# Routing logits of a mixture-of-experts layer taken from the sum ahead of the layer norm

## The chip, the cores and the metric

The kernel runs on one core of one Trainium2 chip, as one program. The metric is device time in microseconds (us), from the start of the program to its end. A run with the hardware profiler gives, beside its time, a trace of what every engine did: TensorE (PE, with its weight loads as PEld), VectorE (DVE), ScalarE (ACT), GpSimd (POOL), and SyncE (SP), which issues most of the DMA transfers.

## The reference

Two transformer layers stand one behind the other. The tensor is 8 x 1024 tokens of 256 values, all in float32. The first layer is an attention over the 16 heads of each token; the second is an attention over the first axis (8 positions, for each of 1024 columns), a layer norm, and a mixture of experts with 8 experts, a capacity of 1024 tokens each, and the best expert for each token. Cut to what matters here:

```python
x  = layernorm(x + first_attention(x))                      # phase A
o  = attention(x)                                           # 4 heads of 64, over 8 positions
y1 = _ln(x + o @ ow.T + ob, ln1_g, ln1_b)                   # eps 1e-5
gates = softmax(y1 @ wg)                                    # wg is 256 x 8
idx   = argmax(gates);  gate_val = gates[idx]
slot  = idx * cap + (rank of the token among those of its expert)   # dropped where rank >= cap
y2 = _ln(y1 + gate_val * expert(idx)(y1), ln2_g, ln2_b)
out = layernorm(x + y2)
```

The logits are `y1 @ wg`. With `s = x + o @ ow.T + ob` for the sum ahead of the norm, mean m and rs = 1/sqrt(var + eps), y1 is `(s - m) * rs * ln1_g + ln1_b`. So with `w = ln1_g * wg` and w centred (the mean over the 256 rows taken off each of its 8 columns), the logits are also `rs * (s @ w) + ln1_b @ wg`: the mean of s falls out, and `s @ w` is the sum of `x @ w`, `o @ (ow.T @ w)` and `ob @ w`.

## The kernel before

The program has three phases. Phase A (`phase_a`) computes the first layer, 64 tiles of 128 tokens, and writes x to DRAM (`x1_d`). Phase B (`phase_b`) computes the second attention, the first norm and the routing. Phase C (`phase_c`) finds each token's place, gathers the rows of each expert, multiplies them, normalises twice and scatters the result.

Phase B works in 8 groups `j` of 128 columns with all 8 positions (`L = 8`), 1024 tokens each. The order of its work is written out by hand. Round `j` has four parts `n`; each computes the attention scores of one quarter (`scores`: matmuls on PE, their maximum `mx` on DVE), the exponentials on ACT (`weights`, two halves), their normalisation (`normed`, DVE), and then, one part later, the turned weights (`turn_s`: transposes on PE, copy `sT` on ACT) and the weighted product (`weighted`: PE, copy `oT` on ACT). Between these steps the list from `fills(j)` is worked off: `some(1)` takes one entry behind the scores, `some(2)` takes two behind the turn, and the rest comes behind `weighted`. In the first part an `output` is held back until `weighted` of the part before is done.

The fills of round j are of two groups. For the next group, `nxt`: `turn_x` turns x with transposes on PE into the PSUM pool `fill` (three buffers) and copies it to `xT` on DVE, in the order that the attention needs; `project_qk` and `project_v` multiply it by the weights. For the group before, `prv`: `output(j, l0)` multiplies two positions of the attention's result by `wout` into one tile of `fill`, POOL makes `xb` = x + out_b (`residual`), DVE adds the two to `r` and takes mean and variance, and POOL makes `rs` (`norm_scalars`). `normal(j, l0)` makes y on DVE, multiplies it by ln1_g and adds ln1_b on POOL, adds ln2_b to x for the later norm on POOL, and sends both rows to `rows_d` in DRAM through SP. `turn_y` turns y on PE and copies it (`yT`) on ACT, `logits` multiplies it by `wg`, and after the last of them `exps` and `choice` compute the softmax, the gate and the expert of the 1024 tokens. `choice` sends the gate column to `rows_d`. `expert_bias` accumulates the bias part of one expert on DVE in rounds 0 to 5; in round 7 the products of two experts are fills.

Each engine works its queue in the order in which the program issues it. A DMA also waits for the transfer eight places before it, which used the same of eight semaphores. Rounds j = -1 (setup: group 0 is turned and projected) and j = 8 (tail: outputs, norms and routing of group 7, with no scores beside them) frame the eight.

Of the kernel before, what the change touches and what calls it, by code (L numbers as in the profile page):

```python
# [24 lines left out]
FP = mybir.dt.float32  # L25
# [8 lines left out]
P = 128  # L34
D = 256
# [14 lines left out]
@with_exitstack  # L50
def fused_kernel(ctx: ExitStack, tc: tile.TileContext, a: dict, out: bass.AP):
    nc = tc.nc

    const = ctx.enter_context(tc.tile_pool(name="const", bufs=1))
    small = ctx.enter_context(tc.tile_pool(name="small", bufs=4))

    ident = const.tile([P, P], FP, name="ident")
    make_identity(nc, ident)
    mhalf = const.tile([P, 1], FP, name="mhalf")
    nc.gpsimd.memset(mhalf, -0.5)  # L60

    dram = ctx.enter_context(tc.tile_pool(name="dram", bufs=1, space=bass.MemoryType.DRAM))
    x1_d = dram.tile([L * N, D], FP, name="x1_d")
    rows_d = dram.tile([L * N, RW], FP, name="rows_d")

    def norm_scalars(r):

        st = small.tile([P, 6], FP, name="st")
        nc.vector.bn_stats(out=st, in_=r)
        mv = small.tile([P, 2], FP, name="mv")  # L70
        nc.vector.bn_aggr(out=mv, in_=st)  # L71
        ve = small.tile([P, 1], FP, name="ve")
        nc.gpsimd.tensor_scalar(ve, mv[:, 1:2], EPS, None, ALU.add)  # L73
        rs = small.tile([P, 1], FP, name="rs")
        nc.gpsimd.tensor_tensor(rs, ve, mhalf, ALU.pow)
        return mv[:, 0:1], rs

    phase_a(tc, a, ident, x1_d, norm_scalars)

    late = ctx.enter_context(tc.tile_pool(name="late", bufs=1))  # L80
    keep = {
        "w12": late.tile([P, DC, E, D], FP, name="w12"),

        "acc": late.tile([P, E, D], FP, name="acc"),
        "hot": late.tile([P, E, NT], FP, name="hot"),
        "gain": late.tile([P, D], FP, name="gain"),
        "red": late.tile([P, NT], FP, name="red"),
    }
    constants(nc, late, keep)
    nc.scalar.dma_start(keep["gain"], a["ln2_g"].partition_broadcast(P))  # L90
    phase_b(tc, a, ident, x1_d, rows_d, keep, norm_scalars)
    phase_c(tc, a, ident, rows_d, keep, out)

# [447 lines left out]
def phase_b(tc, a, ident, x1_d, rows_d, keep, norm_scalars):  # L541
# [8 lines left out]
    with (  # L550
# [15 lines left out]
        for n in ("in_b_v", "out_b", "ln1_g", "ln1_b", "ln2_b"):  # L566
            rows[n] = wp.tile([P, D], FP, name=f"row_{n}")
            nc.scalar.dma_start(rows[n], a[n].partition_broadcast(P))
        wout = wp.tile([P, DC, D], FP, name="wout")
        nc.sync.dma_start(wout, a["out_wT"].rearrange("(c p) f -> p c f", p=P))  # L570
        wg = wp.tile([P, DC, E], FP, name="wg")
        nc.sync.dma_start(wg, a["wg"].rearrange("(c p) e -> p c e", p=P))
        b1 = wp.tile([P, FC, E], FP, name="b1")
# [19 lines left out]
        hot_v = keep["hot"].rearrange("p e (l j) -> p j l e", j=NJ)  # L593
        red_v = keep["red"].rearrange("p (l j) -> p j l", j=NJ)

        def load_x(j):
            G["x", j] = xp.tile([P, L, D], FP, name="x")
            nc.sync.dma_start(G["x", j], x1_v[j])

        def turn_x(j, l0):  # L600
            if l0 == 0:
                G["xT", j] = wp.tile([P, DC, NB, L, B], FP, name="xT")
                G["qk", j] = gp.tile([P, DC, 2, N], FP, name="qk")
            ps = pf.tile([P, 512], FP, name="fill")
            for l in range(2):
                for c in range(DC):
                    n = 2 * l + c
                    nc.tensor.transpose(
                        ps[:, n * P : (n + 1) * P], G["x", j][:, l0 + l, c * P : (c + 1) * P], ident
                    )  # L610
            for l in range(2):
                nc.vector.tensor_copy(
                    G["xT", j][:, :, :, l0 + l, :],
                    ps[:, l * D : (l + 1) * D].rearrange("p (c b n) -> p c b n", c=DC, n=B),
                )
# [118 lines left out]
            )  # L734
            return xb

        def output(j, l0):
            xb = residual(j, l0)
            ps = pf.tile([P, 512], FP, name="fill")
            for l in range(2):  # L740
                for c in range(DC):
                    nc.tensor.matmul(
                        ps[:, l * D : (l + 1) * D],
                        G["oT", j][:, c, l0 + l, :],
                        wout[:, c, :],
                        start=c == 0,
                        stop=c == DC - 1,
                    )
            r = kp.tile([P, 2, D], FP, name="r")
            nc.vector.tensor_tensor(r, ps.rearrange("p (l d) -> p l d", l=2), xb, ALU.add)  # L750
            G["r", j, l0] = r, [norm_scalars(r[:, l, :]) for l in range(2)]

        def normal(j, l0):
            r, sc = G["r", j, l0]
            yx = kp.tile([P, 2, 2 * D], FP, name="yx")
            y = yx[:, :, :D]
            G["y", j, l0] = y
            for l in range(2):
                nc.vector.tensor_scalar(y[:, l, :], r[:, l, :], sc[l][0], sc[l][1], ALU.subtract, ALU.mult)
            both = [P, 2, D]  # L760
# [4 lines left out]
            )  # L765
            nc.sync.dma_start(rows_v[j][:, l0 : l0 + 2, : 2 * D], yx)

        def turn_y(j, l0):
            y = G["y", j, l0]
            ps = pf.tile([P, 512], FP, name="fill")  # L770
            for l in range(2):
                for c in range(DC):
                    n = 2 * l + c
                    nc.tensor.transpose(
                        ps[:, n * P : (n + 1) * P], y[:, l, c * P : (c + 1) * P], ident
                    )
            yT = kp.tile([P, 4, P], FP, name="yT")
            nc.scalar.copy(yT, ps)
            G["yT", j, l0] = yT

        def logits(j, l0):
            yT = G["yT", j, l0]
            ps = pf.tile([P, 512], FP, name="fill")
            for l in range(2):
                for c in range(DC):
                    nc.tensor.matmul(
                        ps[:, l * E : (l + 1) * E],
                        yT[:, 2 * l + c, :],
                        wg[:, c, :],
                        start=c == 0,  # L790
                        stop=c == DC - 1,
                    )
            if l0 == 0:
                G["lg", j] = kp.tile([P, L, E], FP, name="lg")
            nc.vector.tensor_copy(
                G["lg", j][:, l0 : l0 + 2, :], ps[:, : 2 * E].rearrange("p (l e) -> p l e", l=2)
            )

        def over_experts(v):
            return v[:, :, None].to_broadcast([P, L, E])  # L800

        def exps(j):
            lg = G["lg", j]
            top = kp.tile([P, L], FP, name="top")
            nc.vector.tensor_reduce(top, lg, AX.X, ALU.max)
            nc.vector.tensor_tensor(lg, lg, over_experts(top), ALU.subtract)
            nc.scalar.activation(lg, lg, AF.Exp)
# [58 lines left out]
        def fills(j):  # L866
# [8 lines left out]
            def put(part, ok, fn, *args):  # L875
                if ok:
                    o[part].append((fn, *args))

            put(0, N, turn_x, nxt, 0)
            put(0, N, turn_x, nxt, 2)  # L880
            put(0, N, turn_x, nxt, 4)
            put(0, O, output, prv, 0)
            put(0, N, turn_x, nxt, 6)
            put(0, O, output, prv, 2)
            put(0, X, expert_bias, EARLY + j, 0)
            put(0, O, normal, prv, 0)
            put(0, N, project_qk, nxt, 0, 0, 0)
            put(1, O, normal, prv, 2)
            put(1, O, turn_y, prv, 0)
            put(1, O, output, prv, 4)  # L890
            put(1, N, project_qk, nxt, 0, 0, 1)
            put(1, O, logits, prv, 0)
            put(1, O, normal, prv, 4)
            put(1, O, turn_y, prv, 2)
            put(1, X, expert_bias, EARLY + j, 1)
            put(1, N, project_v, nxt, 0)
            put(1, O, logits, prv, 2)
            put(1, N, project_qk, nxt, 0, 1, 0)
            put(2, O, turn_y, prv, 4)
            put(2, O, output, prv, 6)  # L900
            put(2, N, project_qk, nxt, 0, 1, 1)
            put(2, O, logits, prv, 4)
            put(2, O, normal, prv, 6)
            put(2, X, expert_bias, EARLY + j, 2)
            put(2, N, project_v, nxt, 2)
            put(2, N, project_qk, nxt, 1, 0, 0)
            put(2, N, project_v, nxt, 4)
            put(3, O, turn_y, prv, 6)
            put(3, N, project_qk, nxt, 1, 0, 1)
            put(3, N, project_v, nxt, 6)  # L910
            put(3, O, logits, prv, 6)
            put(3, O, exps, prv)
            put(3, X, expert_bias, EARLY + j, 3)
            put(3, N, project_qk, nxt, 1, 1, 0)
            put(3, O, choice, prv)
            put(3, N, project_qk, nxt, 1, 1, 1)
            if j == NJ - 1:
                for n in range(4):
# [449 lines left out]
```

## Time and profile before

| | us |
|---|---|
| runs of the kernel before | 5184.34, 5194.05, 5193.99 |
| median | 5193.99 |
| the profiled execution | 5145.15 |
| its span in the trace | 5143.4 |
| PE busy in the span | 4903.2 (95%) |
| DVE, ACT, POOL busy | 3070.0, 3360.9, 3374.4 |
| mean granted clock of TensorE | 0.977 |

A time in the trace counts from the start of the span. A row of the timeline or of a group gives start or count, duration, engine, line of the kernel, operation, the tile written and the tile read, and in brackets the idle time of the engine ahead of it with what ended that. The granted clock is the share of TensorE's full speed that the throttle let through. L numbers are lines of the kernel before.

### The profile page before, as it was taken

How to read it: one execution, taken by the hardware profiler on the slowest of the kernel's cores; microseconds unless marked ns; L12 is line 12 of the kernel's file. 1: busy time of each engine (PE TensorE's matmuls, PEld its weight loads, DVE VectorE, ACT ScalarE, POOL GpSimd, SP SyncE). 2: the span in 40 equal slices, each digit the busy share in tenths (PEclk: the TensorE clock that was granted, in tenths of full speed). 3: DMA queues.
4: the chain of work that ended last, by engine and by line, in shares of the span. 5: the costliest groups of instructions: out<-in, count | busy, mean ns of one | idle time of the engine just before them, and what ended most of it. 6: DMA issues, size and time to landing. Idle time of an engine off the chain costs nothing. (4 is left out here: it accounts for less than half of the span.)

```text
span 5143.4 us, 189684 instructions
## 1 busy us (share of the span) xinstructions
PE 4903.2 (95%) x79688; PEld 3310.9 (64%) x79688; DVE 3070.0 (60%) x6088; ACT 3360.9 (65%) x4123; POOL 3374.4 (66%) x7014
## 2 busy tenths in 40 slices
PE   7999999999999999999999999999999997889675
PEld 4666666666666666666666666666666664566553
DVE  5665655666566666665666656666666563555467
ACT  5777777777777777777777777777777774444234
POOL 5667667677767767766776776776776764254436
PEclk9999999999999999999999999999999998999787
DMA  2222222222222222222222222222222222132253
GB/s 76 47 48 48 48 48 49 47 49 49 46 48 48 47 48 48 49 47 48 49 47 48 49 46 48 48 48 47 48 49 48 49 47 61 48 76 71 66 182 114
DMA packets 575308, 286.29 MB, mean 56 GB/s; under 512 B 394865, under 2 KB 526065, under 8 KB 574449
## 3 DMA queue, kind: packets, MB, share of 16 engines
q1 hardware_dynamic: 365970, 111.51, 10.9%
q0 software_dynamic: 204800, 159.82, 10.4%
q8 instruction: 623, 10.21, 0.8%
q10 hardware_dynamic: 3680, 2.83, 0.2%
q14 instruction: 235, 1.93, 0.1%
HBM read 72.31 MB, written 33.59 MB: 21 GB/s over the span
## 5 line engine op out<-in xcount | busy, mean ns | idle before, releaser
L359 ACT ACTIVATE e<-pair 128x1024 f32<-128x1024 f32 x3072 | 2977.4, 1021 | 1233.0 <-PE pair L343 1233.0
L403 POOL DMA_DIRECT2D nd<-S x4096 | 1952.9, 484 | 613.3 <-DVE S L393 420.9
L343 PE MATMUL pair<-R,L 32*128 32x128 f32 (+1 forms) x32768 | 1605.6, 322 | 2.0 <-POOL event L314 2.0
L393 DVE COPY S<-sum 128x512 f32<-128x512 f32 x1024 | 707.1, 691 | 1465.9 <-PE sum L382 1153.2
L343 PEld LDWEIGHTS pair<-R,L 32*128 32x128 f32 x32768 | 1271.3, 186 | 48.2 <-POOL event L314 2.6
L373 PE MATMUL sum<-e,V 128*32 128x256 f32 x16384 | 1284.9, 385 | 4.9 <-DVE S L393 4.9
L300 POOL DMA_DIRECT2D R<-qm x2048 | 973.8, 483 | 71.7 <-issue 39.2
L382 PE MATMUL sum<-e,V 128*32 128x128 f32 x16384 | 823.3, 273 | 0.0
L382 PEld LDWEIGHTS sum<-e,V 128*32 128x32 f32 x16384 | 532.8, 110 | 352.2 <-issue 0.9
L373 PEld LDWEIGHTS sum<-e,V 128*32 128x32 f32 x16384 | 406.3, 109 | 236.6 <-DVE qm L267 41.8
L331 PE MATMUL pair<-late,sel 32*128 32x256 bf16 (+1 forms) x6144 | 499.3, 313 | 9.6 <-ACT e L359 9.6
L254 DVE COPY V<-vT 32x128 f32<-32x128 f32 x2048 | 457.4, 223 | 28.1
L412 DVE RECIPROCAL att<-nd 128x256 f32<-128x256 f32 x256 | 447.4, 1748 | 8.0 <-DMA nd<-S 4.1
L331 PEld LDWEIGHTS <-sel 32*128 32x128 bf16 x6144 | 155.4, 91 | 460.4 <-issue 445.0
L314 POOL MEMSET event<- 1x1 f32 x256 | 22.8, 89 | 610.9 <-DMA R<-qm 416.4
L234 PEld LDWEIGHTS ps<-xT,wv 128*128 128x128 f32 x2048 | 238.2, 191 | 44.4 <-issue 41.8
L223 PE MATMUL ps<-wk,xT 128*128 128x512 f32 x512 | 255.3, 621 | 10.9 <-DMA wk<-in_Wk 10.1
L234 PE MATMUL ps<-xT,wv 128*128 128x128 f32 x2048 | 262.6, 281 | 1.6 <-DVE qm L267 0.8
L266 PE MATMUL ps<-wq,xT 128*128 128x512 f32 x512 | 255.7, 622 | 6.7 <-DVE k L224 6.7
L443 PE MATMUL ps<-wo,attT 128*128 128x256 f32 x1024 | 257.9, 395 | 0.7 <-ACT attT L426 0.7
L443 PEld LDWEIGHTS ps<-wo,attT 128*128 128x128 f32 x1024 | 186.1, 191 | 63.7 <-issue 41.8
L73 POOL TENSOR_SCALAR ve<-mv 128x1 f32<-128x1 f32 x128 | 37.9, 296 | 271.6 <-DVE mv L71 270.1
(191 smaller groups left out, 3856.0 us busy)
## 6 DMA issues: line engine op xcount, KB each, us to landing
R<-qm POOLq DMA_DIRECT2D x2048, 32.0 KB, 2.1
nd<-S POOLq DMA_DIRECT2D x4096, 16.0 KB, 1.9
L<-k SPq DMA_DIRECT2D x4088, 8.0 KB
rows_d<-yx SPq DMA_DIRECT2D x32, 512.0 KB
xT<-in_xT SPq DMA_DIRECT2D x64, 128.0 KB
xr<-in_x SPq DMA_DIRECT2D x64, 128.0 KB
x_d<-x1o SPq DMA_DIRECT2D x64, 128.0 KB
x<-x_d SPq DMA_DIRECT2D x8, 1024.0 KB
```

Of the source, the lines that this page charges most:

```text
L234: nc.tensor.matmul(ps[:, i * P : (i + 1) * P], w["v"][:, c, ch * P : (ch + 1) * P], xT_of[t][:, c, :], start=c == 0, stop=c == DC - 1,)
L254: nc.vector.tensor_copy(V[32 * aa : 32 * aa + 32, qd % 2, :, qd // 2, :, aa, 0:4], src[32 * qd : 32 * qd + 32, :, ww, :, aa, :],)
L300: moved.append((None, nc.gpsimd.dma_start(R[:, b, s, b, :], q[:, b, s, cols])))
L331: nc.tensor.matmul(bank[u].rearrange("p (n i) -> p n i", i=n)[:, :, 0:32], sel[pr].rearrange("p a j -> p (a j)"), late[pr, None, :].to_bro ...
L343: one = nc.tensor.matmul(bank[u][:, x * 4 * n : (x + 1) * 4 * n].rearrange("p (b i) -> p b i", i=n), Lt[pr, 2 * (h0 + h) + jb].rearrange(" ...
L359: nc.scalar.activation(e, pair[i], AF.Exp)
L373: nc.tensor.matmul(dst[32 * u : 32 * u + 32], Vs[ww][:, 0, h0 + h, u, :], e0[u // 2][:, u % 2, x * 256 : (x + 1) * 256].rearrange("p (b i) ...
L382: nc.tensor.matmul(dst[32 * u : 32 * u + 32, :, 32:], Vs[ww][:, 1, h0 + h, u, :], e1[u // 2][:, u % 2, h * 128 : (h + 1) * 128].rearrange( ...
L393: nc.vector.tensor_copy(S[:, :, 2 * which : 2 * which + 2, :].rearrange("p b h i -> p h b i"), ps.rearrange("p (h b i) -> p h b i", h=2, b=4),
L403: nc.gpsimd.dma_start(tok[:, b, s, h0 * C1 : (h0 + G) * C1], Sx[:, 4 if s else b, b, :])
L412: nc.vector.reciprocal(att[:, cols], nd[:, 1, cols])
L443: nc.tensor.matmul(ps[:, :D], attT[:, c, :], wo[:, c, :], start=c == 0, stop=c == HID // P - 1)
```

## The change

The logits no longer wait for y. Three parts of the sum ahead of the norm give them:

- `center` and `beside`, new, in the setup: w = ln1_g * wg, centred; `out_w` times w goes as eight further columns beside `out_wT` into `wout`; the two constant rows (out_b and ln1_b through w and wg) go to `wrow`. For this `out_w` and three short columns are loaded.
- `turn_x` also keeps x turned in the plain order (`xl`, a copy on ACT of the same PSUM tile), and `logits_x`, new, multiplies it by w and adds the constant row: the part of the logits that x gives, one round ahead.
- `output` now takes one position l at a time; its product has 256 + 8 columns, and DVE adds the eight to `lg`. `rs` goes to one tile for the group, and `exps` multiplies the logits by it and adds the second constant row.
- `turn_y` and `logits` are gone, and with them the copy `yT`. The order of the fills is new. In the tail `normal` of the last pair comes behind `choice`.

Cut to its core:

```diff
-        wout = wp.tile([P, DC, D], FP, name="wout")
-        nc.sync.dma_start(wout, a["out_wT"].rearrange("(c p) f -> p c f", p=P))
+        wout = wp.tile([P, DC, D + E], FP, name="wout")
+        nc.sync.dma_start(wout[:, :, :D], a["out_wT"].rearrange("(c p) f -> p c f", p=P))
+        outw = wp.tile([P, DC, D], FP, name="outw")
+        nc.sync.dma_start(outw, a["out_w"].rearrange("(c p) f -> p c f", p=P))
+        cols = {}
+        for n in ("ln1_g", "ln1_b", "out_b"):
+            cols[n] = wp.tile([P, DC], FP, name=f"col_{n}")
+            nc.scalar.dma_start(cols[n], a[n].rearrange("(c p) -> p c", p=P), allow_slow_non_contiguous=True)
...
+        def center():
+            w = ww[:, :, 0, :]
+            nc.vector.tensor_tensor(w, wg, column("ln1_g"), ALU.mult)
+            ps = pf.tile([P, 512], FP, name="fill")
+            for c in range(DC):
+                nc.tensor.matmul(ps[:, :E], keep["ones"], w[:, c, :], start=c == 0, stop=c == DC - 1)
+            mean = wp.tile([P, E], FP, name="mean")
+            nc.vector.tensor_scalar(mean, ps[:, :E], 1.0 / D, None, ALU.mult)
+            nc.vector.tensor_tensor(w, w, mean[:, None, :].to_broadcast([P, DC, E]), ALU.subtract)
+            nc.vector.tensor_tensor(ww[:, :, 1, :], w, column("out_b"), ALU.mult)
+            nc.vector.tensor_tensor(ww[:, :, 2, :], wg, column("ln1_b"), ALU.mult)
+
+        def beside():
+            ps = pf.tile([P, 512], FP, name="fill")
+            for k in range(DC):
+                for c in range(DC):
+                    nc.tensor.matmul(ps[:, k * E : (k + 1) * E], outw[:, c, k * P : (k + 1) * P], ww[:, c, 0, :], ...)
+            sums = ps[:, DC * E : (DC + 2) * E]
+            for c in range(DC):
+                nc.tensor.matmul(sums, keep["ones"], ww[:, c, 1:, :].rearrange("p k e -> p (k e)"), ...)
+            nc.vector.tensor_copy(wout[:, :, D:], ps[:, : DC * E].rearrange("p (k e) -> p k e", k=DC))
+            nc.vector.tensor_copy(wrow, sums.rearrange("p (k e) -> p k e", k=2))
...
         def turn_x(j, l0):
...
+            xl = kp.tile([P, 4, P], FP, name="xl")
+            nc.scalar.copy(xl, ps)
+            G["xl", j, l0] = xl
             for l in range(2):
                 nc.vector.tensor_copy(
...
+        def logits_x(j, l0):
...
+                    nc.tensor.matmul(ps[:, l * E : (l + 1) * E], G["xl", j, l0][:, 2 * l + c, :], ww[:, c, 0, :], ...)
+            nc.vector.tensor_tensor(G["lg", j][:, l0 : l0 + 2, :], ps[:, : 2 * E]..., wrow[:, 0:1, :]..., ALU.add)
+
+        def output(j, l):
+            if l == 0:
+                G["rs", j] = gp.tile([P, L], FP, name="rs")
+            if l % 2 == 0:
+                G["r", j, l] = kp.tile([P, 2, D], FP, name="r"), residual(j, l), []
+            r, xb, scalars = G["r", j, l - l % 2]
+            r, xb = r[:, l % 2, :], xb[:, l % 2, :]
+            ps = pf.tile([P, 512], FP, name="fill")
+            for c in range(DC):
+                nc.tensor.matmul(ps[:, : D + E], G["oT", j][:, c, l, :], wout[:, c, :], ...)
+            nc.vector.tensor_tensor(r, ps[:, :D], xb, ALU.add)
+            lg = G["lg", j][:, l, :]
+            nc.vector.tensor_tensor(lg, ps[:, D : D + E], lg, ALU.add)
+            scalars.append(norm_scalars(r, G["rs", j][:, l : l + 1]))
...
         def exps(j):
             lg = G["lg", j]
+            nc.vector.tensor_tensor(lg, lg, over_experts(G["rs", j]), ALU.mult)
+            nc.vector.tensor_tensor(lg, lg, wrow[:, None, 1, :].to_broadcast([P, L, E]), ALU.add)
...
+            last = not N and not X and not 0 <= j < NJ
+            put(0, j < 0, center)
             put(0, N, turn_x, nxt, 0)
             put(0, N, turn_x, nxt, 2)
+            put(0, j < 0, beside)
+            put(0, N, logits_x, nxt, 0)
             put(0, N, turn_x, nxt, 4)
+            put(0, N, logits_x, nxt, 2)
             put(0, O, output, prv, 0)
             put(0, N, turn_x, nxt, 6)
-            put(0, O, output, prv, 2)
+            put(0, O, output, prv, 1)
+            put(0, N, logits_x, nxt, 4)
             put(0, X, expert_bias, EARLY + j, 0)
             put(0, O, normal, prv, 0)
             put(0, N, project_qk, nxt, 0, 0, 0)
+            put(0, N, logits_x, nxt, 6)
+            put(0, O, output, prv, 2)
+            put(1, O, output, prv, 3)
+            put(1, N, project_qk, nxt, 0, 0, 1)
             put(1, O, normal, prv, 2)
-            put(1, O, turn_y, prv, 0)
             put(1, O, output, prv, 4)
-            put(1, N, project_qk, nxt, 0, 0, 1)
-            put(1, O, logits, prv, 0)
-            put(1, O, normal, prv, 4)
-            put(1, O, turn_y, prv, 2)
             put(1, X, expert_bias, EARLY + j, 1)
             put(1, N, project_v, nxt, 0)
-            put(1, O, logits, prv, 2)
+            put(1, O, output, prv, 5)
             put(1, N, project_qk, nxt, 0, 1, 0)
-            put(2, O, turn_y, prv, 4)
+            put(1, O, normal, prv, 4)
             put(2, O, output, prv, 6)
             put(2, N, project_qk, nxt, 0, 1, 1)
-            put(2, O, logits, prv, 4)
-            put(2, O, normal, prv, 6)
+            put(2, O, output, prv, 7)
             put(2, X, expert_bias, EARLY + j, 2)
             put(2, N, project_v, nxt, 2)
+            put(2, O and not last, normal, prv, 6)
             put(2, N, project_qk, nxt, 1, 0, 0)
             put(2, N, project_v, nxt, 4)
-            put(3, O, turn_y, prv, 6)
+            put(3, O, exps, prv)
             put(3, N, project_qk, nxt, 1, 0, 1)
             put(3, N, project_v, nxt, 6)
-            put(3, O, logits, prv, 6)
-            put(3, O, exps, prv)
             put(3, X, expert_bias, EARLY + j, 3)
+            put(3, O, choice, prv)
+            put(3, last, normal, prv, 6)
             put(3, N, project_qk, nxt, 1, 1, 0)
-            put(3, O, choice, prv)
             put(3, N, project_qk, nxt, 1, 1, 1)
```

## The prediction

> **What bounds the kernel now.** I read the busy times by stage first, since the change touches only what lies behind 4331 us.
>
> ```profile
> 0.00:4344.00 4344.00, 4287.01 (x76288) 2863.02 (x76288) 2603.97 (x4953) 3053.31 (x3201) 3019.93 (x6567) 1.00 0.21 49
> ...
> 4436.00:4771.00 335.00, 299.07 (x1904) 215.38 (x1902) 199.31 (x443) 147.95 (x492) 162.48 (x187) 0.94 0.28 72
> ...
> 4834.00:4881.00 47.00, 21.28 (x107) 17.68 (x106) 13.80 (x43) 4.78 (x8) 24.96 (x31) 0.70 0.13 45
> ```
>
> The columns are stage, length, busy time of PE, PEld, DVE, ACT and POOL, granted clock, DMA share and GB/s. The first 4344 us (phase A) are not touched. Phase B is setup to 4377, round 0 to 4422, rounds 1 to 6 of 58.0 us each to 4770, round 7 to 4834, and a tail to 4881 in which PE is idle more than half the time. One round, by its four parts:
>
> ```profile
> 4538.35:4551.82 13.47, 10.95 (x80) 8.03 (x80) 8.53 (x23) 4.99 (x19) 2.79 (x5) 1.00 0.31 20
> 4551.82:4571.25 19.43, 15.50 (x91) 11.36 (x92) 12.43 (x27) 6.95 (x22) 15.09 (x17) 0.82 0.22 68
> 4571.25:4584.65 13.40, 13.40 (x87) 9.99 (x86) 8.08 (x17) 6.94 (x22) 7.22 (x9) 1.00 0.20 61
> 4584.65:4596.32 11.67, 11.67 (x75) 7.72 (x76) 6.65 (x16) 6.52 (x22) 2.52 (x3) 1.00 0.57 157
> ```
>
> PE is full in parts 2 and 3. Part 1 is the slow one: clock 0.82, POOL busy 15 of 19 us. Why, the timeline of PE, DVE and POOL says:
>
> ```profile
> 4553.03 1.09 PE L705 MATMUL sc<-ident,s 128*128 128x128 f32 x8
> 4558.06 1.11 PE L774 MATMUL fill<-ident,yx 128*128 128x128 f32 x4 [3.93 <-POOL yx L762]
> 4558.96 3.62 PE L742 MATMUL fill<-wout,oT 128*128 128x256 f32 x8
> ...
> 4555.06 1.22 DVE L680 TENSOR_REDUCE mx<-sc 128x8 f32<-128x1024 f32 x1
> ...
> 4564.34 0.69 DVE L750 TENSOR_TENSOR r<-fill,xb 128x512 f32<-128x512 f32 x1 [6.19 <-POOL xb L732]
> ...
> 4563.03 1.28 POOL L732 TENSOR_TENSOR xb<-x,row_out_b 128x512 f32<-128x512 f32 x1
> ```
>
> PE waits 3.93 us to turn y, because POOL multiplies it by ln1_g and adds ln1_b first; then eight output records take 3.62 us, against 1.73 for the same eight at 4573.83. DVE waits 6.19 us for xb, which stands on POOL behind two `normal`. It hurts little there: the softmax maximum (L680) is already done. Last, the chain that ends the run:
>
> ```profile
> 4879.81 6.17 DMA rows_d<-gate
> ...
> 4886.74 7.96 DMA w<-in_w
> ...
> 4895.08 10.00 PE pw L1008 x32
> ```
>
> After the routing, the gate column must land before phase C's expert weights are loaded; these, not the routing, end the wait.
>
> **The change, part by part.** All sums are against the profiled execution, 5145.15 us (span 5143.4 and 1.75 around it); the median of the runs shown is 5193.99, 48.8 above. I add the difference to the median. About 0.2%, 10 us, is what a measurement of this kernel can tell from no change.
>
> *Removed from a round:* four turns of y (0.47 us of PE each by starts, 4572.46 to 4572.95: 1.9), with the 3.93 us stall and the slow clock behind it (3.62-1.73 = 1.9). At full clock and without waits a round holds 48.3 us of PE work (10.3, 13.0, 13.35, 11.7); 46.4 remain. *Same amount, moved:* four small products (0.92 each), now on x, one round earlier; four ACT copies (0.59), now xl instead of yT, all in part 0. *Added:* outputs go one l at a time (4 records, 0.87, with 264 columns 0.89), eight tiles of `fill` instead of four on three buffers; DVE pays 0.42+0.17 per l where it paid 0.69 per pair (+2.0 a round, less four 0.16 copies), and two operations of 0.22 in `exps`.
>
> *New wait on ACT.* `turn_x`'s tile is read by ACT (xl) and DVE (xT), and the built program makes each xT copy wait for the xl copy; none of before's xT copies (0.41) waits for ACT. The second xl copy stands behind the softmax's sT copy, so the xT copies stand behind that too. The Trainium skill, PSUM — Partial Sum Buffer, section PSUM bank collisions raise a hardware error, says that two engines may not touch one bank and quadrant at once, reads included; it speaks against this change, and no run here shows it. Overlapped, the copies would save at most 0.59 us a round.
>
> *Moved: the residual add on POOL.* Before, POOL makes xb of pairs 0 and 2 ahead of `normal` 0. Now `output` 2 comes behind `normal` 0, so xb of pair 2 queues behind it on POOL; DVE waits in `output` 2, and behind that wait stand the maximum of part 1's scores, so ACT's exponentials, the copy sT, and PE's weighted product. The same again for pairs 4 and 6. I place one round on the rows, t from its first scores:
> - Exponentials end at 7.15 (before 6.6, plus one xl copy 0.59), `s` is normed at 8.75. DVE then: copies xT 0.75, add 0.17, `output` 0 (0.42+0.17+0.46+0.18 and gaps, 1.25) to 10.95, xT 0.75, `output` 1 to 12.95, add 0.17, two bias steps 1.0, y 0.8: 15.0.
> - POOL: `normal` 0 3.8 to 3.95 (three of 1.27 to 1.39), xb 1.27: 20.2. DVE: `output` 2 to 21.45, maximum 1.22+0.17 and gaps to 22.9. ACT: four exponentials 1.4, sT 1.0. PE's weighted product starts at 25.4; before at 24.2 (4562.51).
> - PE has nothing else: part 0 ends at 15.5 (13.0 of work, 2.4 of gaps on copies), then 1.21+0.89+0.88+1.81 to 20.3. A stall of 5.1 us, and slow clock behind it (1.9, as above). Part 1 ends at 33.8; before 32.9.
> - xb of pair 4: y at 25.5, 3.8+1.27: 30.7. `output` 4 to 32.0, bias 1.0, v 0.69, `output` 5 to 35.0, rs on POOL 1.0, y 0.4, `normal` 4 and xb of pair 6: 41.6. Part 2's weighted product needs the buffer that `output` 6 frees then: 42.35. PE ran out at 39.5: 2.85 us.
> - Then 1.02+1.75+1.81+1.75 and 10.3 of part 3: 59.0 at full clock. I add 1.4 for slow clock and 0.75 because `exps`, now first in part 3, puts four small DVE steps ahead of ACT's exponentials: 61.1.
>
> So +3.1 a round, from +1.0 (no slow clock, no `exps` delay) to +4.6 (bias steps at 0.95 instead of 0.49 beside a busy POOL, as at 4568.78). On the clock: part 0, with 1.72 us of idling, is granted 1.00, part 1, with 3.93, 0.82; a row after 3.03 us (4775.51) takes 1.98 instead of 1.09, so at 2.85 I take slow clock. The Trainium skill, TensorE: Matmul & The Clock Gate, Part 1, throttles only after an idle window of about 3.4 us; the 3.03 us row differs. By the page the 1.4 would go, and rounds 1 to 6 would cost 8 us less.
>
> *Sum over rounds 1 to 6:* 5 x 3.1, and 1 for round 6, which has no bias steps: +16.5 (4 to 25).
>
> *Setup.* `center` fits into the 18.7 us in which PE waits for x. `beside` (12 records) and four products stand between x and the scores of round 0, where PE has no gap: 12 x 0.23 + 4 x 0.92 = 6.4, less 1.9 since the records warm the clock that the first projections now pay (0.67 a record against 0.43): +4.5. Unknown is the load of x: it waits for the last store of phase A, held from 4336.5 to 4340.45 by b1's DMA on its semaphore lane; now acc's small one holds it, but outw's 256 KB and, on ACT's queue, three column loads are added. Nearest rows: 3.9 us (the whole wait gone) and 4.1 us (another landing). So 0 to +8.
>
> *Round 0:* four products, 3.7, in gaps of 6.0 us on xT copies, which the xl copies stretch: +1 (0 to 2). *Round 7* (fills are expert products): turns of y and two stalls (3.0, 2.0 us) go, the xb waits come: -1 (-4 to +2).
>
> *Tail.* Before, from the last xb (4865.3) to `exps` (4878.0) 12.7 us pass with `normal`, turn, copy, products. Now xb (4865.7) is followed by two `output` of 1.15 on DVE and rs 1.0: `exps` at 4869.0, two more small steps, routing done 8.4 us earlier. But `normal` 6 comes behind `choice`: 0.85 of DVE, 3.9 of POOL, then its 512 KB on SP ahead of the expert weights, which wait for it: landing 2.3 (bytes moved at 4877.5) to 6.2 (gate), I take 4.1 as x1's store (4340.45 to 4344.52). Weights leave 9.0 us after the routing instead of 5.5: net -5 (-6.6 to -2.8).
>
> Sum: 16.5 + 4.5 + 1 - 1 - 5 = **+16 us**.
>
> **Rivals.** *The forecast:* POOL's chain takes the place of the turn of y. For it: the built order on POOL and DVE, and the 6.19 us that DVE already waits for xb. *PE work decides:* if xb came in time, a round would be 46.4 plus some 6 of small gaps and clock, 52.5 to 54, 4 us less; 6 x -4, setup +5.5, rest -6: -24, faster. It decides once xb of pair 2 is there before the scores of part 1 end, t = 16.7; it would have to be 3.5 us earlier than my rows put it. For it: PE is busy 51.5 of 58.0. *Even:* the chain as forecast, but each stall too short for the clock and hidden by buffers, +1 a round: 4 + 4.5 + 1 - 1 - 5, some +3. *Load of x late and slow clock throughout:* +35 and more. That the change does not do what it says (no y on PE) the built order rules out.
>
> **How the numbers follow.** Forecast 0.62, late load 0.05, even 0.20, faster 0.13. Time: 5193.99 + 16 = 5210. The low ends add to -7, the high ends to +35, the runs scatter by 10: low 5184 (a tenth below it, the fast case), high 5232. Slower by over 0.2%: 0.67; within: 0.20; faster: 0.13.
>
> **What would show it.** DVE's waits for xb grow from 66 us to over 100; a PE gap of about 5 us in part 1 ahead of the weighted product, released by ACT's sT, and one of about 3 in part 2; rounds of 61 us; routing done some 8 us earlier in the tail. Rounds at or under 56 us, or no DVE wait in `output` 2, would make it wrong.

## The result, and the profile after

The changed kernel takes 5220.55 us (median of five runs, 5211.01 to 5224.28), the kernel before 5191.79 beside it (five runs): ratio 1.0054, 95% interval 1.0043 to 1.0065, 28.8 us slower. The profiled execution took 5224.28 us. Phase C, whose code did not change, takes 293 us in it from the first expert product to the end, and 248 in the profile of before. That goes with the chip: on two of the chips used here it takes some 247 and 290 us in every profile, and the kernel before takes 5145 and 5190. So times are compared by ratios, and traces by stages of phase B.

The busy times by stage: setup, round 0, rounds 1 to 6, tail. Columns as in the prediction: stage, length, busy time of PE, PEld, DVE, ACT and POOL, granted clock, DMA share and GB/s.

```profile
4348.00:4390.78 42.78, 38.14 (x128) 26.98 (x129) 8.12 (x23) 7.15 (x11) 1.27 (x1) 0.70 0.21 63
4390.78:4442.28 51.50, 46.07 (x257) 31.47 (x257) 20.91 (x40) 23.06 (x82) 0.00 (x0) 0.83 0.13 36
4442.28:4809.85 367.57, 306.94 (x1875) 219.39 (x1875) 202.99 (x542) 148.77 (x510) 173.39 (x192) 0.94 0.26 66
...
4873.96:4911.60 37.64, 13.00 (x57) 8.98 (x55) 13.28 (x51) 2.44 (x4) 21.62 (x28) 0.70 0.12 42
```

Rounds 1 to 6 take 61.3 us on average (58.0 before), round 0 51.5 (45.1), the tail up to the end of the routing 37.6 (46.6). From x landing (4353.57) to the first scores 37.2 us pass (27.0). One round by its four parts:

```profile
4566.98:4583.08 16.10, 13.40 (x109) 11.00 (x109) 11.43 (x37) 7.81 (x24) 2.90 (x5) 1.00 0.25 18
4583.08:4600.90 17.82, 13.21 (x72) 9.04 (x73) 8.23 (x22) 4.98 (x19) 12.87 (x14) 0.90 0.24 74
4600.90:4617.26 16.36, 13.83 (x76) 9.93 (x76) 8.68 (x24) 6.35 (x21) 10.09 (x12) 0.90 0.16 49
4617.26:4628.62 11.36, 10.40 (x63) 6.38 (x62) 6.57 (x14) 5.70 (x21) 3.14 (x3) 1.00 0.56 162
```

PE, full in parts 2 and 3 before, now has idle time in all four. The timeline of all engines says why, in order of time:

```profile
4585.99 1.26 POOL L786 TENSOR_TENSOR xb<-x,row_out_b 128x512 f32<-128x512 f32 x1
...
4587.29 0.42 DVE L824 TENSOR_TENSOR r<-fill,xb 128x256 f32<-128x256 f32 x1 [4.93 <-POOL xb L786]
...
4588.31 1.19 DVE L734 TENSOR_REDUCE mx<-sc 128x8 f32<-128x1024 f32 x1
...
4591.19 1.02 ACT L761 COPY sT<-sc 128x1024 f32<-128x1024 f32 x1
...
4592.26 1.98 PE L771 MATMUL fill<-sT,v 128*64 128x128 f32 x16 [4.22 <-ACT sT L761]
...
4608.63 0.42 DVE L824 TENSOR_TENSOR r<-fill,xb 128x256 f32<-128x256 f32 x1 [3.80 <-POOL xb L786]
...
4609.27 1.98 PE L771 MATMUL fill<-sT,v 128*64 128x128 f32 x16 [2.53 <-DVE lg L826]
```

POOL makes xb of pair 2 behind `normal` 0; DVE waits 4.93 us for it, and only then takes the maximum of scores that ended at 4584.4; ACT's exponentials and its copy sT follow, and PE, idle for 4.22 us, starts the weighted product at half speed (1.98 against 1.09). In part 2 the same wait, 3.80 us, holds the PSUM buffer that the weighted product needs. Over phase B, DVE waits 91.7 us for xb (66.4 before; over 100 were forecast).

In the chain that ends last, behind a routing that is done 9.0 us sooner, stand the last rows, then the expert weights:

```profile
4916.11 3.97 DMA rows_d<-yx
...
4920.15 5.93 DMA w<-in_w1T
4926.09 3.22 issue
4929.30 9.23 PE pw L1058 x32
```

### The profile page after: what moved, and what is told of

Its sections match the earlier page's. It is cut to its first block, busy times and chain, and to the rows that moved or that the text cites. A ratio compares the mean times of both kernels' runs of the same rounds, so it can differ in the third digit from the quotient of the medians.

```text
span 5222.5 us, 189653 instructions
## 1 busy us (share of the span) xinstructions
PE 4921.3 (94%) x79576; PEld 3318.2 (64%) x79576; DVE 3069.6 (59%) x6207; ACT 3357.2 (64%) x4123; POOL 3379.8 (65%) x7014
```

## Experiments

The runs came in three sets: e1 to e4; c0, b1, e6 and e7; e5, f2, f3 and f4. All ratios are to the kernel before in the same set (5145.44, 5190.12 and 5190.35 us); 0.001 is 5.2 us. Gains in us are worked out from the ratios; a difference of two medians can be some us off them. Lengths of rounds, parts and the setup are from each run's profile, and the lines in its rows are those of its own kernel.

**c0_changed: the changed kernel again.**

> The changed kernel itself once more, unaltered, as the anchor of the variants beside it: ratio to the kernel before 1.004 to 1.007, rounds of 61 us, and the time behind the tail (from the first expert product of phase C to the end) within 2 us of the other variants, since phase C is the same code. If the ratio is under 1.003, the loss depends on more than the order of the work.

5217.9 us, ratio 1.0059 (1.0046 to 1.0072). Rounds 1 to 6: 61.0 us; phase C from its first product 289.5, the others of this set 289.6 to 292.2. It repeats the result.

**e1_residual: xb one pair earlier.**

```diff
             if l == 0:
...
+                G["xb", j, 0] = residual(j, 0)
             if l % 2 == 0:
-                G["r", j, l] = kp.tile(...), residual(j, l), []
+                if l < 6:
+                    G["xb", j, l + 2] = residual(j, l + 2)
+                G["r", j, l] = kp.tile(...), G["xb", j, l], []
```

> The changed kernel, but the residual add of the next pair (xb of pairs 2, 4, 6) is issued on POOL at the start of the pair before, ahead of that pair's `normal`. Theory (xb behind `normal` on POOL sets the stalls): DVE's waits for xb in `output` fall from 91.7 us to under 30, PE's gaps on sT in part 1 (4.2) and on lg in part 2 (2.5) shrink below 2, rounds 1 to 6 go from 61.3 to 53-57 us, and the time falls by 25 to 45 us against the changed kernel (5221 to 5176-5196, at or under the kernel before). Rival (the xT copies behind the xl copy, and the slow clock after any gap): rounds stay at 60-62 us and the time within 5 us of the changed kernel. Second rival (the wait only moves to rs, which then stands behind `normal` on POOL and is awaited by y): the gaps shrink by half, rounds 58-60, time 8 to 18 us less.

5139.86 us, ratio 0.9984 (0.9975 to 0.9993): 0.0070 to 0.0075 less than the changed kernel's two ratios, 36 to 39 us. No wait for xb is left; the one wait of `r` in the rounds is for its product on PE (view: waits, rounds 1 to 6; total us, times, longest):

```profile
DVE r L827 <- PE fill L824: 15.2, 18, 1.9
```

Part 1 falls from 17.8 to 12.0-12.9 us, part 2 from 16.4 to 13.4, rounds to 57.1 on average. Against the profile of the result, rounds 1 to 6 give 25 us, and round 7 and the tail some 5 each. The theory holds; its second rival does not (DVE waits 12.9 us in all for rs). But part 3 grew from 11.4 to 13-15 us. Its timeline:

```profile
4598.42 1.32 POOL L841 TENSOR_TENSOR yx<-x,row_ln_b 128x512 f32<-128x512 f32 x1
4598.65 1.17 DVE L852 TENSOR_TENSOR lg<-lg,wrow 128x64 f32<-128x64 f32 x1
...
4599.70 2.48 POOL L786 TENSOR_TENSOR xb<-x,row_out_b 128x512 f32<-128x512 f32 x2
4599.86 0.22 DVE L854 TENSOR_REDUCE top<-lg 128x8 f32<-128x64 f32 x1
4600.11 0.94 DVE L855 TENSOR_TENSOR lg<-lg,top 128x64 f32<-128x64 f32 x1
...
4603.69 1.09 PE L771 MATMUL fill<-sT,v 128*64 128x128 f32 x16 [2.77 <-ACT sT L761]
```

The steps of `exps` stand ahead of ACT's exponentials, and two of them take 1.17 and 0.94 us where they take 0.22 in the changed kernel: they now meet POOL's last `normal` and the early xb. The Trainium skill, SBUF — State Buffer, section Who interferes with whom, says that a VectorE instruction with two SBUF inputs contends with a GpSimd one that reads SBUF, through a shared port, and that one with a single SBUF input, outside the two-port modes, does not; the rows agree (1.17 and 0.94 for two inputs, 0.22 for `top` between them).

**b1_residual: the same edit in the kernel before.**

```diff
-            xb = residual(j, l0)
+            if l0 == 0:
+                G["xb", j, 0] = residual(j, 0)
+            if l0 < 6:
+                G["xb", j, l0 + 2] = residual(j, l0 + 2)
+            xb = G["xb", j, l0]
```

> The kernel before, with the same edit as e1_residual: xb of the next pair issued on POOL ahead of the `normal` of the pair before. Theory 1 (the changed kernel's gain with xb early, 33 us, is only the repair of its own new wait; before, xb for pairs 4 and 6 was late but hidden): time within 5 us of the kernel before, rounds 57 to 58. Theory 2 (the early xb is worth as much without the logits change, whose own gain is then nil or negative): DVE's waits for xb fall from 66 us to under 15, the rounds to 54 to 56, time 12 to 25 us less than the kernel before.

5161.46 us, ratio 0.9953 (0.9941 to 0.9965): 24 us faster than the kernel before by the ratio; rounds of 55.3 us, no wait for xb. The second theory is right, and this is the fastest version of the study. So the order of xb is worth 24 us without the logits change too. With that order in both, the change still costs 0.0031, some 16 us, so POOL's chain is not the whole loss. Up to the first product of phase C, by stages of the two traces (e1 against b1): setup 37.0 against 27.2, round 0 48.4 against 45.1, rounds 1 to 6 342.8 against 331.6, round 7 and tail 108.8 against 114.0.

**e5_no_ln2b: a shorter chain on POOL.**

```diff
-            yx = kp.tile([P, 2, 2 * D], FP, name="yx")
-            y = yx[:, :, :D]
+            y = kp.tile([P, 2, D], FP, name="yx")
...
-            nc.gpsimd.tensor_tensor(yx[:, :, D:], G["x", j]..., rows["ln2_b"]..., ALU.add)
-            nc.sync.dma_start(rows_v[j][:, l0 : l0 + 2, : 2 * D], yx)
+            nc.sync.dma_start(rows_v[j][:, l0 : l0 + 2, :D], y)
+            nc.sync.dma_start(rows_v[j][:, l0 : l0 + 2, D : 2 * D], G["x", j][:, l0 : l0 + 2, :])
```

> The changed kernel with one of the three POOL operations of `normal` (1.27 us of 3.8) gone: ln2_b isn't added (that part of the computation is left out), and x goes to its place in the rows by a DMA of its own. Theory (the length of POOL's chain ahead of xb sets the stalls of parts 1 and 2): DVE's waits for xb (4.9 and 3.8 us) and the PE gaps behind them (4.2 and 2.5) shrink by about 1.3 us each, with less slow clock behind them: rounds 1 to 6 from 61.3 to 57.5-59, ratio to the kernel before 1.000 to 1.003 instead of 1.006. Rival (DVE's own work in parts 1 and 2, two steps per position, sets them): rounds stay within 1 us of 61.3.

This version leaves out the addition of ln2_b and sends x by a second DMA. 5196.77 us, ratio 1.0012 (1.0003 to 1.0021); rounds 58.8 us, DVE's longest wait for xb 3.7 instead of 4.9. With 1.27 us less on POOL per pair, parts 1 and 2 together take 28 to 29 us instead of 34.2 in rounds 1 to 5. But the round as a whole gains only 2.2 to 2.4 us, since part 0 grows from 16 to 18-21: there DVE waits for w2 ahead of `choice` and the maximum, and PE then waits 3.60 us for sT. In round 2:

```profile
4499.59 1.01 DVE L905 SCALAR_TENSOR_TENSOR acc<-w,b,acc 128x256 f32<-128x256 f32 x2 [1.99 <-DMA w<-in_w]
...
4506.40 1.98 PE L771 MATMUL fill<-sT,v 128*64 128x128 f32 x16 [3.60 <-ACT sT L761]
```

So the dose shows in the parts where it was forecast; that the round's total fell in the forecast range is in part luck.

**e3_swap: the xT copies ahead of the xl copy.**

```diff
-            xl = kp.tile([P, 4, P], FP, name="xl")
-            nc.scalar.copy(xl, ps)
-            G["xl", j, l0] = xl
             for l in range(2):
                 nc.vector.tensor_copy(G["xT", j]..., ps...)
+            xl = kp.tile([P, 4, P], FP, name="xl")
+            nc.scalar.copy(xl, ps)
+            G["xl", j, l0] = xl
```

> The changed kernel, but in `turn_x` the two xT copies on DVE come ahead of the xl copy on ACT, which then waits for them. Rival to the forecast (the copies of the shared tile set the loss): DVE's waits for xl (21.1 us) go, part 0's gaps with them, rounds fall by 2 us or more, time 12 us less or better. Forecast's theory (the stalls of parts 1 and 2 are POOL's, and gaps of part 0 pass into the wait of part 1): the gaps in parts 1 and 2 stay at 4 and 2.5 us, rounds within 1 us of 61.3; ACT now waits for DVE ahead of the exponentials, so the time is between 3 us less and 12 us more.

5193.07 us, ratio 1.0081 (1.0068 to 1.0095); rounds 64.5 us, part 0 20 instead of 16. DVE no longer waits for xl, but ACT waits 38.7 us in the rounds for the copies on DVE, ahead of its exponentials. The rival is out: parts 1 and 2 stay at 17.4 and 16.4 us. The forecast that the round would stay within 1 us missed too. The shared tile costs less in the order that the change chose than in the other; what it costs at all, no version without it shows.

**e2_setup: the setup's products last.**

```diff
-            xl = kp.tile([P, 4, P], FP, name="xl")
+            xl = (kp if j else wp).tile([P, 4, P], FP, name="xl" if j else f"xl_{l0}")
...
-            put(0, j < 0, beside)
-            put(0, N, logits_x, nxt, 0)
+            put(0, N and j >= 0, logits_x, nxt, 0)      # likewise 2, 4, 6
...
+            put(3, j < 0, beside)
+            for l0 in range(0, L, 2):
+                put(3, j < 0, logits_x, 0, l0)
```

> The changed kernel, but in the setup `beside` and the four products of group 0 stand behind its projections instead of among them (xl of group 0 in four buffers of its own). Theory (they cost more than forecast because they run at the slow clock, 1.72-1.85 us for eight records against 0.92, and hold the projections back): from x landing to the first scores 37.2 us falls to 32-35, time 3 to 5 us less than the changed kernel. Rival (the clock rises a fixed time after PE starts, whatever it works on, so that the projections pay instead): the 37.2 stays within 1 us, time the same within 2.

5176.32 us, ratio 1.0055 (1.0041 to 1.0069): the time does not tell it from the changed kernel. In the trace the setup takes 31.0 us instead of 37.2 (34.2 in c0). The granted clock (last column but two) shows what the small products do. First the changed kernel, in which they stand among the turns and projections:

```profile
4358.00:4362.00 4.00, 4.00 (x21) 4.00 (x22) 1.12 (x5) 0.58 (x1) 0.00 (x0) 0.50 0.01 2
...
4366.00:4370.00 4.00, 4.00 (x12) 2.55 (x11) 0.13 (x1) 0.69 (x1) 0.00 (x0) 0.50 0.00 0
```

and e2, in which 44 of them run one behind the other from 4377.83 to 4383.15:

```profile
4374.00:4378.00 4.00, 4.00 (x14) 2.04 (x12) 0.69 (x1) 0.69 (x1) 0.00 (x0) 1.00 0.01 4
4378.00:4382.00 4.00, 4.00 (x38) 4.00 (x38) 0.66 (x5) 0.69 (x1) 0.00 (x0) 1.00 0.02 4
4382.00:4386.00 4.00, 4.00 (x29) 3.67 (x29) 0.78 (x3) 0.00 (x0) 0.00 (x0) 0.53 0.00 0
```

PE is busy without a gap in all of these rows. In the changed kernel the clock stays at half until some 20 us after x has landed (14 us in c0; before: full 8 us after it); in e2 it rises early, and then falls while PE works on products with 8 or 16 columns: the first scores behind them take 1.92 us instead of 1.05, and part 0 of round 0 18.7 instead of 17.6. The setup gets shorter, but the products take the slow clock along.

**e4_tail: the last `normal` ahead of `exps`.**

```diff
-            put(2, O and not last, normal, prv, 6)
+            put(2, O, normal, prv, 6)
...
-            put(3, last, normal, prv, 6)
```

> The changed kernel, but in the tail `normal` of the last pair stands in part 2, ahead of `exps`, as in the other rounds. Theory (landing of the last rows, 4.0 us and POOL's 3.9 us ahead of it, holds the expert weights back by 3 us): routing is done 1 to 3 us later, the weights leave 4 to 6 us after it instead of 8.6, time 0 to 3 us less. Rival (the wait of `exps` behind y costs what the landing saves): time 0 to 2 us more.

5181.23 us, ratio 1.0068 (1.0054 to 1.0081), 5 to 7 us over the changed kernel's two ratios, at the edge of what the intervals separate. The weights leave 61.3 us after the last scores (59.2 and 58.1 in the changed kernel's two traces): only 8.0 us behind the routing, but the routing is later, since `exps` stands behind y, which waits for rs, and two of its steps take 1.25 and 1.05 us beside POOL's `normal`. The rival is right: from the last turn of scores to phase C's first product 57.2 us pass instead of 55.3. What the time has beyond these 1.9 us is not explained; in this profile rounds 1 to 6, which the edit does not touch, take 62.2 us.

**e6_exps and e7_more: `exps` later; `choice` later.**

```diff
-            put(3, O, exps, prv)
             put(3, N, project_qk, nxt, 1, 0, 1)
             put(3, N, project_v, nxt, 6)
             put(3, X, expert_bias, EARLY + j, 3)
+            put(3, O, exps, prv)
```

> e1_residual, and `exps` goes from the head of part 3 to behind its bias steps (where the kernel before had it). Theory (with xb early, the last stall is part 3: five small DVE steps of `exps`, lengthened beside a busy POOL from 0.2 to as much as 1.2 us, stand ahead of ACT's exponentials and give a PE gap of 3 us on sT): part 3 falls from 14.6 to 11.4-12.2 us, rounds 1 to 6 from 57.1 to 54-55.5, time 10 to 20 us less than e1_residual. Rival (the delay passes to part 0 of the next round, where `choice` then stands ahead of the maximum): part 3 falls but part 0 grows by as much, rounds 56.5 to 58, time within 4 us.

5200.78 us, ratio 1.0019 (1.0010 to 1.0028), slower than e1. Part 3 falls to 10.9 us as expected, but part 0 grows to 25. In round 1, ahead of which no rows were sent, part 0 takes 15.4 us and the round 51.8; from round 2 on the timeline of DVE shows this:

```profile
4556.22 1.00 DVE L911 SCALAR_TENSOR_TENSOR acc<-w,b,acc 128x256 f32<-128x256 f32 x2 [6.34 <-DMA w<-in_w]
```

With `exps` gone from the head of part 3, the bias step slipped ahead of `normed`, and waits for w2, whose load SP issues behind the last rows and the load of x. The edit moved more than it said. This wait is not all of it: in f2, below, it is gone and part 0 still takes 22.

e7 adds the setup of e2, keeps the logits `lg` in four tiles of their own, and:

```diff
+            put(1, prv > 0, choice, prv - 1)
...
-            put(3, O, choice, prv)
+            put(3, last, choice, prv)
```

> e6_exps, and `choice` goes from part 3 into part 1 of the next round (the tail's stays), and the setup's products behind its projections as in e2_setup. Theory: `choice` (eight DVE steps, 2.0 us) no longer delays the maximum of part 0's scores by some 1.2 us, so part 0 falls by about 1; the setup saves 6 us: 8 to 14 us less than e6_exps. Rival (POOL and DVE in part 1 have no room; `choice` there only moves the delay to part 1): only the setup's 3 to 6 us.

5199.17 us, ratio 1.0022 (1.0013 to 1.0030): the setup gives 6 us and part 0 4 a round, but part 2 takes 3.5 more, so that rounds stay at 59.8, and round 7 and the tail take 4.7 and 2.0 more. Theory and rival are not told apart while the bias steps wait (34 us).

**f2_loads, f3_v6 and f4_setup: from e1 on, one by one.** In f2 `exps` comes behind the projections, and w2 is loaded a part ahead:

```diff
-            put(3, O, exps, prv)
             put(3, N, project_qk, nxt, 1, 0, 1)
             put(3, N, project_v, nxt, 6)
+            put(3, N, project_qk, nxt, 1, 1, 0)
+            put(3, O, exps, prv)
             put(3, X, expert_bias, EARLY + j, 3)
             put(3, O, choice, prv)
             put(3, last, normal, prv, 6)
-            put(3, N, project_qk, nxt, 1, 1, 0)
...
-                    if j < E - EARLY:
-                        load_expert(EARLY + j, n, False)
+                    if j == 0 and n == 0:
+                        load_expert(EARLY, 0, False)
+                    e, piece = divmod(4 * j + n + 1, 4)
+                    if e < E - EARLY:
+                        load_expert(EARLY + e, piece, False)
```

> e1_residual with `exps` behind `normed` of part 3 (two projections ahead of it on PE), and each load of an expert's w2 for the bias steps issued one part earlier. Theory (e6 failed because the bias step of part 3 then stood on DVE ahead of `normed` and waited up to 7.4 us for w2, which SP issues behind the last rows and the load of x): DVE's waits for w fall from 40.5 us (e6) and 12.8 (e1) to under 5, part 3 is 11 to 11.5 us, part 0 15 to 16, rounds 1 to 6 52 to 53.5 us, ratio to the kernel before 0.992 to 0.995. Rival (the w2 transfer itself is late, 40 us a round of DMA traffic): DVE waits over 20 us, rounds 56 or more, ratio 0.998 or more.

5180.58 us, ratio 0.9986 (0.9977 to 0.9995). The waits for w2 are gone and part 3 is 10.4 us, but part 0 takes 22, except in round 1 (16.2): rounds 57.0, as in e1. The rival's numbers came (rounds over 56, ratio over 0.998), but not by its cause, since DVE no longer waits for w2; the theory's sum is out too. What holds part 0 is a PE gap of 4.3 us ahead of its weighted product.

In f3:

```diff
+            put(0, 0 < j < NJ, project_v, j, 6)
             put(0, N, turn_x, nxt, 0)
...
-            put(3, N, project_v, nxt, 6)
+            put(3, j < 0, project_v, nxt, 6)
```

> f2_loads with the last `project_v` of a group moved from part 3 to the head of part 0 of its own round, in place of the first turn of x. Theory (in part 0 PE lacks 2.4 us of work ahead of sT, and the xl copy ahead of the exponentials costs ACT 0.6): the gap on sT in part 0 falls under 1 us and the slow clock behind it goes, part 0 plus part 3 falls by 1 to 3 us, rounds 50 to 52, ratio 0.988 to 0.993. Rival (the turned x then comes later and the gap passes to the first projection of part 0): rounds within 0.5 us of f2.

5178.62 us, ratio 0.9979 (0.9970 to 0.9988); rounds 56.6. Part 3 falls by 1.2, part 0 stays at 22 to 24: the gap shrinks from 4.3 to 2.4 us, not under 1, and the slow clock stays. Rounds 1 and 2 stand side by side here. Stages of part 0, first without and then with a `choice` ahead of it:

```profile
4438.00:4454.00 16.00, 15.29 (x115) 12.62 (x114) 10.82 (x30) 7.81 (x24) 2.74 (x5) 1.00 0.00 1
...
4489.00:4511.00 22.00, 19.53 (x114) 16.36 (x111) 13.51 (x40) 7.71 (x24) 3.17 (x6) 0.77 0.16 34
```

and PE in the two:

```profile
4443.32 1.09 PE L771 MATMUL fill<-sT,v 128*64 128x128 f32 x16 [0.39 <-ACT sT L761]
...
4496.17 1.32 PE L771 MATMUL fill<-sT,v 128*64 128x128 f32 x16 [2.42 <-ACT sT L761]
4497.54 1.84 PE L798 MATMUL fill<-ww,xl 128*128 128x8 f32 x8
```

`choice` ends part 3 on DVE with eight steps of 0.2 to 0.3 us, and the maximum starts 2 us late. The 2 us become a gap of 2.42, the clock falls to half, and stays there for the small products, turns and outputs that follow, until some 4506: 2 us cost 6. That `choice` is the cause is read from the trace; a version with it elsewhere and with w2 in time was not tried.

f4 adds the edit of e2 to f3.

> f3_v6 with the setup's products behind its projections, as in e2_setup: from x landing to the first scores 37 us falls to 31, ratio 0.001 lower than f3_v6. If the slow clock only passes into round 0: the same as f3_v6.

5172.23 us, ratio 0.9969 (0.9957 to 0.9981): the best with the change, 16 us faster than the kernel before, and by its ratio 8 us behind b1, though the two intervals overlap. From x to the scores 33.0 us (f3: 36.9).

## Why the prediction was right, and where its sizes were off

Slower was forecast, by 16 us, for POOL's chain behind `normal`; measured are 28.8. By its terms, with the profile of the result and c0:

| term | predicted | measured |
|---|---|---|
| setup, x landing to first scores | +4.5 (0 to 8, with the load of x) | +10.2; c0 +7.2 |
| round 0 | +1 (0 to 2) | +6.4; c0 +5.1 |
| rounds 1 to 6 | +16.5 (4 to 25) | +19.7; c0 +18.3 |
| round 7 | -1 (-4 to +2) | 0.0; c0 -2.5 |
| tail to the first product of phase C | -5 (-6.6 to -2.8) | -5.5; c0 -5.5 |

*The round* held step by step. From the first scores (4566.98) the weighted product of part 1 was put at 25.4 and came at 25.3; part 1's end at 33.8, came at 33.9; part 2's product at 42.35, came at 42.3; the round's end at 61.1, came at 61.6. The stalls, 5.1 and 2.85, were 4.22 and 2.53. e1 takes the cause away and the stalls go, e5 shortens it and parts 1 and 2 shrink. Of the 3.2 us by which the term was too small, 2.2 are round 1, whose part 0 took 18.0 us; c0, where it took 15.4, has +18.3. One reading was off: the 3.62 us of the slow output records were set beside 1.73, which is the same eight by starts; their record has 1.89, so the slow clock there costs 1.7, not 1.9.

*The setup and round 0* are the terms that were mis-sized, by 5.7 and 5.4 us (c0: 2.7 and 4.1); the whole forecast missed by 13. The setup had "12 x 0.23 + 4 x 0.92 = 6.4, less 1.9 since the records warm the clock". `beside` took 2.7, as put; but the four products took 1.85, 1.71, 1.71 and 1.72, together 7.0 instead of 3.7 (6.2 in c0, where the clock came up ahead of the last), and warmed nothing: two projections among them still took 3.75 us instead of 1.88. Before, the same two took 5.35 together at the start, and all behind them ran at full clock. In round 0 the same products run at 1.85 and 1.72 behind a gap of 3.8. The line from before:

```profile
4354.73 5.35 PE L623 MATMUL fill<-xT,wi 128*128 128x512 f32 x8 [0.89 <-PE fill L608]
```

and those from the changed kernel:

```profile
4357.76 1.85 PE L798 MATMUL fill<-ww,xl 128*128 128x8 f32 x8
...
4364.58 3.75 PE L677 MATMUL fill<-xT,wi 128*128 128x512 f32 x4
4368.12 1.72 PE L798 MATMUL fill<-ww,xl 128*128 128x8 f32 x8
4369.69 3.76 PE L677 MATMUL fill<-xT,wi 128*128 128x512 f32 x4
...
4398.78 1.85 PE L798 MATMUL fill<-ww,xl 128*128 128x8 f32 x8 [3.81 <-DVE lg L805]
```

The term took the price of a small product from rows at full clock, and took for granted that any record of PE keeps the clock up. The changed kernel ran some 20 us at half clock with PE busy (c0 14), and e2 lost the clock with no idle time at all. The Trainium skill, TensorE: Matmul & The Clock Gate, Part 1, would not have helped: it has the clock rise after some 3.4 us of activity, whatever is issued in it, and fall after an idle window of that length. The measurement decides.

*The wait on ACT* that the prediction weighed (xT copies behind the xl copy) is there, 21.1 us in all; e3 shows that the other order is worse. *The tail* went as worked out: routing 9.0 us earlier (8.4 forecast), the last rows landing in 3.97 us (4.1), weights leaving 8.6 us after the routing (9.0); e4 adds that the place of `normal` 6 was nevertheless the better one.

*The rival "PE work decides"* named the right point, xb in time, but not the size: e1 is 36 to 39 us below the changed kernel and 8 below the kernel before, where 24 were worked out. Its 52.5 to 54 us a round allowed for no new wait; behind xb stood `exps`, then w2, then, by the trace, `choice`, each behind the one before.

*The load of x*, which the prediction left between 4 us less and 4 us more, came at almost nothing. x lands 3.4 us later in the changed kernel's profile (1.5 to 7.4 in its variants), but 3.2 of these stand already in the first load that SP issues for phase B (`wout`, at 4334.77 instead of 4331.60); from there to x landing 18.8 us pass instead of 18.6 (19.3 in c0). Open is why that point comes later, when phase A is the same code; the two profiles of the kernel before and b1 agree within 0.2 us.

## What to carry over

Before moving a step to another place in a list, follow every engine's queue that it feeds: here one POOL addition of 1.27 us, issued behind a chain of 3.8 instead of ahead of it, cost the changed kernel 36 to 39 us, and its early issue alone was worth 24 us to the kernel before. Then compare like with like: with the early issue in both, the change still cost 16 us. When a stall is repaired, look for the next wait behind it, and for what else the edit shifts in the queue; three repairs in a row gave back what they won. Price small matmuls by what they do to the clock, not by their time at full clock.

## What the runs showed of the hardware

- Products with 8 to 16 columns did not hold or raise the granted clock: 0.50 over 16 us of PE busy time in the setup of the changed kernel (14 in c0), and a fall from 1.00 to 0.53 within a run of 44 of them in e2.
- In rounds 0 to 7 of all fourteen profiles, PE gaps of up to 2.28 us left the weighted product behind them at 1.09 us in 284 of 311 cases, gaps of 2.42 to 2.54 in 6 of 38, and gaps of 2.62 to 3.04 in 12 of 22, so the length of the gap does not decide alone. In part 0, where small products, turns and outputs follow, the clock was then granted 0.77 over 22.0 us (f3) and 0.82 over 19.2 (e1), which is 10 and 7 us at half speed.
- Two DVE steps with two SBUF inputs of 128x64 took 0.94 to 1.25 us instead of 0.22 beside POOL's additions.
- The same phase C took 247 to 248 us on one chip and 290 to 292 on another.
